# Halo rows copied by ScalarE, a tile per channel block, a fourth product buffer, a bank of its own for the back transposes and a new order, in a Restormer block

## The chip, the core and the metric

The kernel runs on one core of a Trainium2 chip. The metric is the device time of one launch in microseconds (us). Below, PE is TensorE, DVE is VectorE, ACT is ScalarE, POOL is GpSimd and SP is SyncE, as in the profile.

## The reference

The input `x` has 16 images of 128 channels by 96 by 96 pixels, all in float32. One transformer block is applied: attention over channels, and then a feed-forward network with a depthwise 3x3 convolution.

```python
xn1 = layernorm(x_hwc, ln1_w, ln1_b)                 # over the 128 channels of a pixel
x = x + attention(xn1, wq, wk, wv, wp)               # 8 heads; a 16x16 softmax per head, over all 9216 pixels
xn2 = layernorm(x_hwc, ln2_w, ln2_b)
h1 = einsum('bchw,oc->bohw', xn2, w_in)              # 128 -> 512 channels
h2 = conv2d(h1, w_dw, 3x3, padding=1, groups=512)    # depthwise: nine taps for each channel
x = x + einsum('bchw,oc->bohw', gelu(h2), w_out)     # 512 -> 128 channels
```

## The kernel before

Channels lie on the 128 partitions. An image is cut into 8 bands of 12 rows (1152 pixels), and a band into 3 units of 4 rows (384 pixels). Over the images run two normalising passes and the feed-forward network, all overlapped: while image i goes through the network, the second norm (`b`) of image i and the first norm (`a`) of image i+1 are prepared.

**A norm.** For each group of 4 x 128 pixels PE transposes pixels to partitions (`pT`, L495), DVE takes statistics (`st`, L501) and a variance (`ve`, L508), POOL raises it to the power -0.5 (`rstd`, L512), DVE makes a shift (`nb`, L516), ACT scales (`zT`, L535), and PE transposes back (`pB`, L571). ACT puts that into a padded image `xn` of 98 rows (L575 for `b`, with weight and bias columns; L579 for `a`, which also adds up the row sums of a unit). For pass `a` PE also accumulates the Gram matrix of `zT` (L545). Attention is then a chain of small steps on 128 x 128 matrices, since queries and keys are linear in that Gram matrix and in the pixel sums. The mixed result (`pm`, L456) is evacuated by ACT (L465), and a DMA that adds brings in `x` (L468).

**The network.** The 512 hidden channels are 4 blocks. For three of them, and in some bands for the fourth too, a band is a *job*: PE makes 14 rows of hidden values (`ph`, L756), ACT copies them into a padded tile `h1` (L761), and then the nine taps are shared out. ACT makes the first product into `h3` (L772) and two more into product tiles `pr` (also L772). DVE adds six taps into `h3`, one instruction of 1152 elements each (L776, called taps below). POOL issues two adding DMAs (L780): the first adds one `pr` tile to the other (the *pr add*), the second adds that sum to `h3` (the *h add*). ACT then applies the gelu (L784). For the fourth block (`PE_CHUNK`), in the bands that `by_pe` names, PE does the whole convolution instead, with nine matmuls for each unit on weights composed of `w_in` and a tap (`pc`, L829), and ACT applies the gelu from PSUM (L835). The output product (`po`, L852) adds up the four blocks, DVE adds it to `x` (L859), and SP stores.

The first two rows of a job's `h1` tile are the last two rows of the same block's job one band earlier. Before the change SP moves them by DMA: `keep_halo` (L752) saves rows 12 and 13 of `h1` into a tile `halo`, and `take_halo` (L749) brings them into rows 0 and 1 of another `h1` tile. Three `h1` tiles go round among all jobs.

**Buffers.** Of the 8 PSUM banks two hold `pT`, one the Gram matrix, and five go round among `ph`, `pc`, `po`, `pm` and `pB`. In SBUF there are 3 `pr` tiles, 9 `h3` tiles, 3 `zT` tiles, 6 band tiles `xb` and 2 band tiles `x1`.

**The order.** Each engine runs its instructions in the order written. That order comes from a planner in the kernel: each kind of work has a place number (`AT`, plus a step within a job) and rough durations, a list schedule over engines and buffers is played through, and the work is emitted in the order of its starts. It sets an order alone; the waits at run time are semaphores.

Of the kernel before, what the change touches and what calls it, by code (L numbers as in the profile page):

```python
# [9 lines left out]
F32 = mybir.dt.float32  # L10
# [15 lines left out]
AT = dict(  # L26
    weights=3.75, zeros=6.85, load_a=-9.5, forth_a=-1.65, stats_a=-6.65, variance_a=-4.05, power_a=1.6,
    shift_a=2.3, scaled_a=3.2, gram=2.15, back_a=-10.4, place_a=-5.35, attention=-6.3, mix=-6.6,
    residual=-4.9, mixed=-6.6, add_x=-2.1, forth_b=-5.75, stats_b=0.35, variance_b=-10.5, power_b=-15.05,
    shift_b=-8.65, scaled_b=0.5, back_b=-14.1, place_b=-5.75, take_halo=1.4, hidden=-0.6, kept=0.4,  # L30
    keep_halo=6.55, product=-2.75, products=1.25, add_last=-9.3, tap=3.3, add_first=11.25, gelu=-5.7,
    conv=2.8, conv_gelu=0.1, out=2.85, add=-1.65, store=1.5,
# [6 lines left out]
T_ADD, T_MOVE, T_HALO = 3100, 1800, 400  # L39
# [157 lines left out]
def tile_restormer_block(  # L197
# [33 lines left out]
    HP, WP = H + 2, W + 2  # L231
# [10 lines left out]
    p_h = ctx.enter_context(tc.tile_pool(name="p_h", bufs=5, space=PSUM))  # L242
    p_g = ctx.enter_context(tc.tile_pool(name="p_g", bufs=1, space=PSUM))

    xbs, x1s = {}, {}

# [22 lines left out]

    wqkT = const.tile([P, 2 * P], F32, name="wqkT")  # L270
# [8 lines left out]
    xns = [pad.tile([P, HP, WP], F32, tag=f"xn{k}", name=f"xn{k}") for k in range(min(B, 2))]  # L279
    small = ctx.enter_context(tc.tile_pool(name="small", bufs=4))  # L280
    xhp = ctx.enter_context(tc.tile_pool(name="xhp", bufs=3))
# [8 lines left out]
    h1s = [h1p.tile([P, BR + 2, WP], F32, name=f"h1_{k}") for k in range(H1_BUFS)]  # L290
    halos = [h1p.tile([P, 2, WP], F32, name=f"halo_{n}") for n in range(NCH) if n != PE_CHUNK]

    def interior(i, u):
        return xns[i % 2][:, 1 + u * UR : 1 + (u + 1) * UR, 1 : 1 + W]
# [4 lines left out]
    def x_unit(of, i, u):  # L299
# [3 lines left out]
    grams, sums, mats, h3s, staged = {}, {}, {}, {}, {}  # L303
    plan = Plan(
        tr=2, h=5, g=1, batch=4, zT=3, x1=X1_BUFS, xb=XB_BUFS, h1=H1_BUFS, pr=PR_BUFS, h3=H3_BUFS
# [3 lines left out]
    def at(kind, place):  # L309
        return place + AT[kind]  # L310

# [14 lines left out]

    def pe(ns, p, f, r, w):
        op("PE", ns, p, f, r, w, ns + 200 + SLACK, ns)
# [4 lines left out]
    def add(p, f, r, w):  # L333
        op("POOL", 950, p, f, r, w, 500 + SLACK, dma=T_ADD)
# [7 lines left out]
    def zeros(p):  # L342


        def around(t, r):
            for k in (0, r - 1) if r == HP else ():
                nc.gpsimd.memset(t[:, k, :], 0.0)
            for k in (0, WP - 1):
                nc.gpsimd.memset(t[:, :, k : k + 1], 0.0)

        for t, r in [(xns[0], HP)] + [(t, BR + 2) for t in h1s] + [(xn, HP) for xn in xns[1:]]:
            op("POOL", 1000, at("zeros", p), lambda t=t, r=r: around(t, r), [], [("w", "in")], 1200)

    def weights(p):

        mine = [("h3", ("weights", k)) for k in range(2)]
        v, banks = staged, iter(range(99))
# [13 lines left out]
        def transposed(parts, kept, gives):  # L371

            bank = ("h", ("weights", next(banks)))
            d = {}

            def forth():
                d["pt"] = p_h.tile([P, 4 * P], F32, tag="h", name=f"pw_{bank[1][1]}")
# [3 lines left out]
            pe(440, at("weights", p), forth, mine, [bank])  # L381
            dve(700, at("weights", p), lambda: kept(d["pt"]), [bank], [("w", g) for g in gives] + mine[1:])
# [6 lines left out]
        def biases():  # L389
            v["pc"] = p_h.tile([1, 2 * P], F32, tag="h", name="pc")  # L390
            nc.tensor.matmul(v["pc"], lhsT=b1, rhs=v["wqkT"], start=True, stop=True)

        def comp_parts(ts):
# [4 lines left out]

        op("ACT", 400, at("load_a", p), loads, [], mine, 900 + SLACK, dma=2 * T_MOVE)
        transposed(  # L400
# [6 lines left out]
            lambda pt: nc.vector.tensor_copy(winT.rearrange("p n c -> p (n c)"), pt), ["in"],  # L407
# [5 lines left out]
        for t0 in (0, 4, 8):  # L413
# [4 lines left out]
                lambda pt, ts=ts: nc.vector.tensor_copy(  # L418
                    comp[:, ts[0] : ts[-1] + 1, :].rearrange("p t c -> p (t c)"), pt[:, : len(ts) * P]
# [20 lines left out]
    def norm(i, second, place_of):  # L440
# [8 lines left out]
        def x2(s, u):  # L449
# [4 lines left out]
            def mix():  # L454
                pm = d["pm"] = p_h.tile([P, UT], F32, tag="h", name=f"pm_{i}_{u}")
# [26 lines left out]
        def pixels(s, q):  # L482
# [4 lines left out]
            pool, key_ = (p_h, "h") if early else (p_tr, "tr")  # L487
            by_dve = QT // 2 if early else 0

            def forth():  # L490
                d["pT"] = pool.tile([P, QT, P], F32, tag=key_, name=f"pT_{name}_{q}")
# [28 lines left out]
            def take_zT():  # L520
                zTs[q] = xhp.tile([P, QT, P], F32, tag="zT", name=f"zT_{name}_{q}")

            def also_scaled():
                for j in range(by_dve):
                    nc.vector.tensor_scalar(
                        zTs[q][:, j, :], d["pT"][:, j, :], d["mv"][:, j, 1:2], d["rstd"][:, j : j + 1],
# [3 lines left out]
            def scaled():  # L530
# [3 lines left out]
                for j in range(by_dve, QT):  # L534
                    nc.scalar.activation(  # L535
                        zT[:, j, :], d["pT"][:, j, :], AF.Identity,
# [3 lines left out]
            def gram():  # L540
                if q == 0:
                    grams[i] = p_g.tile([P, 4 * P], F32, tag="g", name=f"g_{i}")
                for t in tiles:
                    zt = zTs[q][:, t - tiles[0], :]
                    nc.tensor.matmul(  # L545
                        grams[i][:, :P], lhsT=zt, rhs=zt, start=(t == 0), stop=(t == NU * TPU - 1)
# [13 lines left out]
            if not second:  # L560
                pe(QT * 220, at("gram", s), gram, [(*zt, 0), (*zt, 1)], [("g", i)])

        def channels(s, u):
# [3 lines left out]
            def back():  # L567
                d["pB"] = p_h.tile([P, UT], F32, tag="h", name=f"pB_{name}_{u}")
                for j in range(TPU):
                    q, k = divmod(u * TPU + j, QT)  # L570
                    nc.tensor.transpose(d["pB"][:, j * P : (j + 1) * P], zTs[q][:, k, :], ident)  # L571
# [363 lines left out]
```

## Time and profile before

| what | value |
|---|---|
| median of three runs (lowest, highest) | 4548.23 us (4544.1, 4552.64) |
| the profiled execution's own time | 4542.75 us |
| its span | 4541.0 us |
| busy: PE, DVE, ACT, POOL | 4395.3, 4278.3, 4033.9, 1851.5 us |
| DMA queues' share of 16 engines: adding DMAs on POOL's queue, others | 68.0%, 14.3% |
| bytes moved by DMA | 806.84 MB |

Busy time on PE is the time covered by matmuls whose ends are modelled; successive ones overlap, so it overstates what PE needs. A row of a list of groups reads: source line, engine, operation, output and inputs, their shapes, count, then busy us, the mean ns of one, the idle time before it and what ended that. A row of a timeline reads: start in us, length in us, engine, line, operation, and a count where several like instructions in a row are merged. A row of the waits reads: who waited, for whom, total us, number of times, longest us.

### The profile page before, as it was taken

The numbers are of one execution on the slowest core, as the hardware profiler recorded it, in microseconds if no ns is written. First come the engines' busy times: TensorE is split into PE (matmuls) and PEld (weight loads), VectorE is DVE, ScalarE is ACT, GpSimd is POOL, SyncE is SP. The second block draws the span as 40 slices with busy tenths as digits, with TensorE's granted clock in tenths as the row PEclk, the third lists the DMA queues.
The fourth block names the chain that finished last, engine by engine and source line by source line (L and its number), as shares of the span: only waits on it lengthen the run. The fifth ranks groups of instructions, "written<-read, shape, count | busy, mean of one in ns | idle before, by whom it ended". The sixth has DMA issues, their size and how long they took to land.

```text
span 4541.0 us, 55504 instructions
## 1 busy us (share of the span) xinstructions
PE 4395.3 (97%) x17974; PEld 2798.1 (62%) x17974; DVE 4278.3 (94%) x5671; ACT 4033.9 (89%) x7100; POOL 1851.5 (41%) x1606
## 2 busy tenths in 40 slices
PE   7999999999999999999999999999999999999998
PEld 5666656666666665666666666666666656666554
DVE  6999999999999999999999999999999999999988
ACT  4889889899898998989999998998989989899876
POOL 2334434344344444434334343443444434344331
PEclk9999999999999999999999999999999999999999
DMA  2878888898898888888888888888988888888887
GB/s 71 175 172 182 175 181 187 177 195 175 174 195 181 191 173 180 192 170 182 184 183 188 179 187 178 183 178 174 198 179 174 183 182 185 184 183 173 172 171 159
DMA packets 279124, 806.84 MB, mean 178 GB/s; under 512 B 31920, under 2 KB 119344, under 8 KB 278832
## 3 DMA queue, kind: packets, MB, share of 16 engines
q0 software_dynamic: 142560, 583.99, 68.0%
q1 hardware_dynamic: 133920, 218.49, 14.3%
q8 instruction: 142, 2.33, 0.2%
q14 instruction: 150, 1.23, 0.1%
q10 hardware_dynamic: 2352, 0.81, 0.1%
HBM read 148.26 MB, written 75.50 MB: 49 GB/s over the span
## 4 chain that ended last, share of the span: by engine, by line
PE 35%; DMA 26%; DVE 15%; ACT 13%; issue 7%; POOL 4%; POOLq 0%; ACTq 0%; DVEq 0%
DMA pr<-pr 18%; DVE h L776 12%; PE pc L829 11%; PE po L852 8%; DMA h<-pr 7%; PE ph L756 6%; ACT pr L772 4%; PE g L545 2%; ACT h L772 2%; PE pm L456 2%; ACT zT_b L535 1%; DMA x<-in_x_dram 1%; ACT h L784 1%; ACT h L761 1%; PE pB_a L571 1%
## 5 line engine op out<-in xcount | busy, mean ns | idle before, releaser
L776 DVE SCALAR_TENSOR_TENSOR h<-h,dw,h 128x1152 f32<-128x1152 f32 x2612 | 3647.0, 1411 | 68.3 <-ACT h L772 57.9
L829 PE MATMUL pc<-xn,comp 128*128 128x384 f32 x4158 | 1490.3, 487 | 6.4 <-ACT x L465 2.1
L772 ACT ACTIVATE pr<-h,dw 128x1152 f32<-128x1152 f32 x868 | 1104.7, 1283 | 82.9 <-DMA pr<-pr 81.8
L852 PE MATMUL po<-h,woutT 128*128 128x384 f32 x3072 | 1124.6, 489 | 20.4 <-ACT h L784 12.1
L829 PEld LDWEIGHTS pc<-xn,comp 128*128 128x128 f32 x4158 | 766.1, 190 | 498.9 <-issue 8.2
L756 PE MATMUL ph<-xn,winT 128*128 128x384 f32 (+1 forms) x2610 | 1005.0, 503 | 30.9 <-ACT h L761 8.5
L780 POOL DMA_DIRECT2D h<-pr x434 | 395.6, 912 | 1509.7 <-DMA pr<-pr 420.3
L852 PEld LDWEIGHTS po<-h,woutT 128*128 128x128 f32 x3072 | 564.9, 190 | 399.2 <-ACT h L784 23.6
L756 PEld LDWEIGHTS ph<-xn,winT 128*128 128x128 f32 x2610 | 475.3, 190 | 369.8 <-issue 40.3
L784 ACT ACTIVATE h<-h 128x1152 f32<-128x1152 f32 (+1 forms) x437 | 516.9, 1183 | 188.9 <-DMA h<-pr 186.7
L761 ACT COPY h<-ph 128x384 f32<-128x384 f32 (+1 forms) x1305 | 616.5, 531 | 63.8 <-PE ph L756 59.5
L512 POOL TENSOR_TENSOR rstd_b<-ve_b,mhalf 128x4 f32<-128x4 f32 x288 | 506.7, 1769 | 374.5 <-DVE ve_b L508 357.2
L512 POOL TENSOR_TENSOR rstd_a<-ve_a,mhalf 128x4 f32<-128x4 f32 x288 | 505.5, 1755 | 319.0 <-DVE ve_a L508 300.7
L772 ACT ACTIVATE h<-h,dw 128x1152 f32<-128x1152 f32 x435 | 560.7, 1290 | 7.6 <-PE po L852 2.6
L780 POOL DMA_DIRECT2D pr<-pr x434 | 412.3, 950 | 319.6 <-ACT pr L772 274.0
L535 ACT ACTIVATE zT_b<-pT_b,nb_b,rstd_b 128x128 f32<-128x128 f32 x1142 | 438.7, 496 | 28.7 <-DVE nb_b L516 16.8
L535 ACT ACTIVATE zT_a<-pT_a,nb_a,rstd_a 128x128 f32<-128x128 f32 x1116 | 427.4, 490 | 18.8 <-DVE nb_a L516 10.5
L456 PE MATMUL pm<-xn,mwT 128*128 128x384 f32 x768 | 300.8, 493 | 11.6 <-ACT xn L575 4.3
L545 PE MATMUL g<-zT_a 128*128 128x128 f32 x2304 | 308.7, 278 | 0.0
L545 PEld LDWEIGHTS g<-zT_a 128*128 128x128 f32 x2304 | 285.6, 194 | 3.8
L575 ACT ACTIVATE xn<-pB_b,b,w 128x384 f32<-128x384 f32 x384 | 259.4, 706 | 15.8 <-PE pB_b L571 15.4
L501 DVE BATCH_NORM_STATS2 st_a<-pT_a 128x6 f32<-128x256 f32 x576 | 243.5, 426 | 20.3 <-PE pT_a L495 19.7
(97 smaller groups left out, 3173.0 us busy)
## 6 DMA issues: line engine op xcount, KB each, us to landing
pr<-pr POOLq DMA_DIRECT2D x434, 576.0 KB, 6.8
h<-pr POOLq DMA_DIRECT2D x434, 576.0 KB, 5.1
x<-in_x_dram SPq DMA_DIRECT2D x128, 576.0 KB, 5.7
out_dram<-x SPq DMA_DIRECT2D x127, 576.0 KB, 5.0
x<-in_x_dram POOLq DMA_DIRECT2D x122, 576.0 KB, 8.2
halo<-h SPq DMA_DIRECT2D x336, 98.0 KB, 4.2
h<-halo SPq DMA_DIRECT2D x336, 98.0 KB, 4.5
out_dram<-x SPq DMA_DIRECT2D x3, 192.0 KB, 1.9
```

What stands on the lines that cost most here:

```text
L456: nc.tensor.matmul(rows(pm), lhsT=mats[i][0], rhs=interior(i, u), start=True, stop=True)
L512: nc.gpsimd.tensor_tensor(rstd, d["ve"], mhalf, ALU.pow)
L535: nc.scalar.activation(zT[:, j, :], d["pT"][:, j, :], AF.Identity, bias=d["nb"][:, j : j + 1], scale=d["rstd"][:, j : j + 1],)
L545: nc.tensor.matmul(grams[i][:, :P], lhsT=zt, rhs=zt, start=(t == 0), stop=(t == NU * TPU - 1))
L756: nc.tensor.matmul(ph, lhsT=winT[:, n, :], rhs=xn[:, r0 + r : r0 + e, 1 : 1 + W], start=True, stop=True)
L761: nc.scalar.copy(h1_tile()[:, r:e, 1 : 1 + W], d.pop(("ph", r)))
L772: nc.scalar.activation(to, window(t), AF.Copy, scale=dw[:, n, t : t + 1])
L776: nc.vector.scalar_tensor_tensor(h3, window(t), dw[:, n, t : t + 1], h3, ALU.mult, ALU.add)
L780: nc.gpsimd.dma_start(out=to, in_=d["pr", t], accum_op=ALU.add)
L784: nc.scalar.activation(h3, h3, AF.Gelu)
L829: nc.tensor.matmul(d["pc"], lhsT=comp[:, t, :], rhs=xn[:, r0 + dy : r0 + dy + UR, dx : dx + W], start=(t == 0), stop=(t == 8),)
L852: nc.tensor.matmul(rows(d["po"]), lhsT=woutT[:, n, :], rhs=h3s[g, n][:, s * UR : (s + 1) * UR, :], start=(k == 0), stop=(k == NCH - 1),)
```

## The change

Six things are changed together.

1. **Halo rows by ACT.** Each channel block has an `h1` tile of its own (four in all). After a job, ACT copies rows 12 and 13 of the tile onto rows 0 and 1 of the same tile (336 copies of 2 x 96 elements). Both halo DMAs are gone, so SP only loads and stores. A row of the padded tiles has 97 elements in place of 98: the right pad of a row is the left pad of the next.
2. **Four product tiles** `pr` in place of three; five band tiles `xb` in place of six.
3. **Sums by a ones column.** `zT` has a 129th column of ones, so that the Gram matmul also gives the pixel sums. The placing of `pB` for pass `a` becomes a plain copy, and the accumulator reads and a DVE reduction per image go.
4. **Weight of the second norm folded into `w_in` and the composed weights** once at the start; the placing for pass `b` keeps one column (the bias) and loses the other.
5. **PSUM.** `pB` gets one bank of its own, and four banks go round among the rest.
6. **Another order, and fewer bands on PE.** New place numbers; the planner reckons an adding DMA's result 900 ns later than it did. PE convolves the fourth block in 73 of 128 bands (4 of every 7) in place of 77 (3 of every 5), so there are 439 jobs in place of 435.

```diff
-PE_BANDS = (1, 2, 4)
+PE_BANDS = (0, 2, 4, 6)
+PE_OF = 7
-X1_BUFS, XB_BUFS, H1_BUFS, PR_BUFS, H3_BUFS = 2, 6, 3, 3, 9
-IN_TURN = ("tr", "h3", "h1", "pr", "xb", "x1")
+H_BANKS = 4
+X1_BUFS, XB_BUFS, PR_BUFS, H3_BUFS, ZT_BUFS = 2, 5, 4, 9, 3
+IN_TURN = ("tr", "h3", "pr", "xb", "x1")
...
-    h1s = [h1p.tile([P, BR + 2, WP], F32, name=f"h1_{k}") for k in range(H1_BUFS)]
-    halos = [h1p.tile([P, 2, WP], F32, name=f"halo_{n}") for n in range(NCH) if n != PE_CHUNK]
+    h1s = [h1p.tile([P, (BR + 2) * WP + 2], F32, name=f"h1_{n}") for n in range(NCH)]
+    zT_bufs = [h1p.tile([P, QT, P + 1], F32, name=f"zT_{k}") for k in range(ZT_BUFS)]
+    def window(t, r, n, dx=0):
+        return t[:, r * WP + dx : (r + n) * WP + dx].rearrange("p (r w) -> p r w", w=WP)[:, :, :W]
...
-        op("POOL", 950, p, f, r, w, 500 + SLACK, dma=T_ADD)
+        op("POOL", 950, p, f, r, w, 1400 + SLACK, dma=T_ADD)
...
-                        grams[i][:, :P], lhsT=zt, rhs=zt, start=(t == 0), stop=(t == NU * TPU - 1)
+                        grams[i][:, : P + 1], lhsT=zt[:, :P], rhs=zt, start=(t == 0), stop=(t == NU * TPU - 1)
...
-                d["pB"] = p_h.tile([P, UT], F32, tag="h", name=f"pB_{name}_{u}")
+                d["pB"] = p_bk.tile([P, UT], F32, tag="bk", name=f"pB_{name}_{u}")
...
-                    nc.scalar.activation(interior(i, u), rows(d["pB"]), AF.Identity, bias=b2, scale=w2)
+                    nc.scalar.activation(interior(i, u), rows(d["pB"]), AF.Identity, bias=b2)
...
-                nc.scalar.activation(
-                    interior(i, u), rows(d["pB"]), AF.Identity, accum_out=sums[i][:, u : u + 1]
-                )
+                    nc.scalar.copy(interior(i, u), rows(d["pB"]))
...
-        def take_halo():
-            nc.sync.dma_start(out=h1_tile()[:, :2, :], in_=halos[n])
-        def keep_halo():
-            nc.sync.dma_start(out=halos[n], in_=h1_tile()[:, BR : BR + 2, :])
+        def halo():
+            nc.scalar.copy(window(h1_, 0, 2, 1), window(h1_, BR, 2, 1))
...
+        if to_halo:
+            act(t_copy(2 * W), at("halo", j), halo, h1[3:], h1[:1])
```

How the order moves is seen at three places. In the names, `pr_60_2_1` is product tile 1 of band 60, block 2; `h3_60_2` is that job's accumulator; `rstd_b7_15` is the power for group 15 of image 7 in pass `b`.

On POOL, about half way through the program, this stands before:

```order
L780 DMA pr_60_2_1_17406<-pr_60_2_2_17463 128x1152
L512 TENSOR_TENSOR rstd_b7_15_17500<-ve_b7_15_17494,mhalf_86 128x4
L780 DMA h3_60_2_17372<-pr_60_2_1_17406 128x1152
L780 DMA pr_60_3_1_17511<-pr_60_3_2_17529 128x1152
L512 TENSOR_TENSOR rstd_a8_16_17547<-ve_a8_16_17542,mhalf_86 128x4
L780 DMA h3_60_3_17446<-pr_60_3_1_17511 128x1152
```

and this after:

```order
L807 DMA pr_59_1_1_15571<-pr_59_1_2_15584 128x1152
L807 DMA h3_59_0_15436<-pr_59_0_1_15471 128x1152
L550 TENSOR_TENSOR rstd_b7_11_15613<-ve_b7_11_15597,mhalf_93 128x4
L550 TENSOR_TENSOR rstd_a8_16_15660<-ve_a8_16_15646,mhalf_93 128x4
L807 DMA pr_59_2_1_15643<-pr_59_2_2_15653 128x1152
L503 DMA x2_7_6_15619<-in_x_dram 128x1152
L807 DMA h3_59_1_15554<-pr_59_1_1_15571 128x1152
```

Before, a job's h add (`h3`) stands one to two rows behind its own pr add; after, the pr add of the next job has come in between. Over the whole program another job's pr add lies between a job's two adds in 13 of 434 jobs before, and in 365 of 438 after.

On DVE, in bands 56 and 57, this stands before (its first pair of taps starts at 2084.70 us of the profile):

```order
L776 SCALAR_TENSOR_TENSOR h3_57_0_16283<-h1_2_134,dw_98,h3_57_0_16283 128x1152
L776 SCALAR_TENSOR_TENSOR h3_56_2_16173<-h1_1_133,dw_98,h3_56_2_16173 128x1152
L516 SCALAR_TENSOR_TENSOR nb_a8_3_16401<-st_a8_3_16354,rstd_a8_3_16387 128x4
L776 SCALAR_TENSOR_TENSOR h3_57_0_16283<-h1_2_134,dw_98,h3_57_0_16283 128x1152
L501 BN_STATS st_b7_7_16412<-pT_b7_7_16371 128x6
L776 SCALAR_TENSOR_TENSOR h3_57_0_16283<-h1_2_134,dw_98,h3_57_0_16283 128x1152
L501 BN_STATS st_b7_7_16412<-pT_b7_7_16371 128x6
L776 SCALAR_TENSOR_TENSOR h3_57_0_16283<-h1_2_134,dw_98,h3_57_0_16283 128x1152
L508 TENSOR_SCALAR ve_b7_7_16434<-st_b7_7_16412 128x4
L776 SCALAR_TENSOR_TENSOR h3_57_1_16420<-h1_0_132,dw_98,h3_57_1_16420 128x1152 x2
```

and in band 56 after:

```order
L803 SCALAR_TENSOR_TENSOR h3_56_1_14763<-h1_1_138,dw_105,h3_56_1_14763 128x1152
L539 BN_STATS st_a8_7_14849<-pT_a8_7_14837 128x6
L803 SCALAR_TENSOR_TENSOR h3_56_0_14681<-h1_0_137,dw_105,h3_56_0_14681 128x1152
L554 SCALAR_TENSOR_TENSOR nb_b7_5_14860<-st_b7_5_14811,rstd_b7_5_14842 128x4
L539 BN_STATS st_a8_7_14849<-pT_a8_7_14837 128x6
L803 SCALAR_TENSOR_TENSOR h3_56_0_14681<-h1_0_137,dw_105,h3_56_0_14681 128x1152
L546 TENSOR_SCALAR ve_a8_7_14872<-st_a8_7_14849 128x4
L803 SCALAR_TENSOR_TENSOR h3_56_1_14763<-h1_1_138,dw_105,h3_56_1_14763 128x1152
L803 SCALAR_TENSOR_TENSOR h3_56_0_14681<-h1_0_137,dw_105,h3_56_0_14681 128x1152
```

Taps of two jobs alternate oftener, so a tap stands less often right behind a tap on the same `h3` tile (`x2`, as in the last row of the first piece): 275 such pairs in the whole program before, 123 after. Taps right behind a tap on another tile: 460 before, 634 after.

On ACT, in bands 61 to 63, this stands before around a gelu (`h3_62_0<-h3_62_0`):

```order
L772 ACTIVATE h3_62_2_17881<-h1_0_132,dw_98 128x1152
L835 ACT_TABLE_LOAD
L835 ACTIVATE h3_62_3_17886<-pc_62_0_17813 128x384
L772 ACTIVATE pr_62_1_2_17898<-h1_2_134,dw_98 128x1152
L761 COPY h1_1_133<-ph_63_0_2_17896 128x4x96
L761 COPY h1_1_133<-ph_63_0_6_17901 128x4x96
L784 ACTIVATE h3_62_0_17722<-h3_62_0_17722 128x1152
L772 ACTIVATE pr_62_2_1_17921<-h1_0_132,dw_98 128x1152
L761 COPY h1_1_133<-ph_63_0_10_17905 128x4x96
```

and in bands 60 and 61 after:

```order
L799 ACTIVATE pr_60_2_2_15954<-h1_2_139,dw_105 128x1152
L788 COPY h1_0_137<-h_1_77 128x4x96
L788 COPY h1_0_137<-h_3_79 128x4x96
L779 COPY h1_0_137<-h1_0_137 128x2x96
L788 COPY h1_0_137<-h_0_76 128x4x96
L799 ACTIVATE h3_61_0_15982<-h1_0_137,dw_105 128x1152
L779 COPY h1_1_138<-h1_1_138 128x2x96
L811 ACT_TABLE_LOAD
L811 ACTIVATE h3_60_0_15762<-h3_60_0_15762 128x1152
L799 ACTIVATE pr_61_0_1_16015<-h1_0_137,dw_105 128x1152
```

Two halo copies (L779) stand among the copies from PSUM now. Between a job's second `pr` product and its gelu stand 17 rows in the median before and 26 after.

More of the change, by code (lines that the diff above doesn't have):

```diff
@@ L310, in at, with bank @@
         return place + AT[kind]
+    def bank(key, n=4 * P):
+        return banks[plan.slot["h", key]][:, :n]
     def z_units(i, r0, r1):
@@ L356, in weights @@
         mine = [("h3", ("weights", k)) for k in range(2)]
-        v, banks = staged, iter(range(99))
+        v, names = staged, iter(range(99))
         def loads():
@@ L520, in take_zT @@
             def take_zT():
[L521 removed]
+                zTs[q] = zT_bufs[plan.slot["zT", (name, q)]]
             def also_scaled():
@@ L788, in conv_job @@
         left = [t for t in range(1, 9) if t not in dma_taps]
-        h1 = [("h1", jn, r) for r, _ in chunks]
+        h1 = [("h1", n, k) for k in range(4)]
         h3 = [("h3", jn, s) for s in range(UPB)]
-        after = []
-        if from_halo:
-            after = [("h1", jn, "halo")]
-            move(at("take_halo", j), take_halo, [("halo", n)], after, T_HALO)
         for k, (r, e) in enumerate(chunks):
@@ L850, in product @@
             if k == 0:
-                d["po"] = p_h.tile([P, UT], F32, tag="h", name=f"po_{g}_{s}")
+                d["po"] = bank(("out", g, s), UT)
             nc.tensor.matmul(
```

138 lines of the change are left out of this document (76 added, 62 removed).

## The prediction

> **What bounds the kernel now.** I read the page's head first, then the windows, then who waited for whom on DVE, and last what holds ACT and POOL.
>
> ```profile
> span 4541.0 us, 55504 instructions
> PE 4395.3 (97%) x17974; PEld 2798.1 (62%) x17974; DVE 4278.3 (94%) x5671; ACT 4033.9 (89%) x7100; POOL 1851.5 (41%) x1606
> 1000.00:1500.00 500.00, 490.95 (x2026) 314.03 (x2025) 478.12 (x632) 457.68 (x807) 211.44 (x178) 1.00 0.84 181
> 3500.00:4000.00 500.00, 488.07 (x1988) 307.69 (x1988) 471.73 (x622) 452.00 (x796) 206.50 (x177) 1.00 0.84 180
> ```
>
> The windows (PE, PE loads, DVE, ACT, POOL, granted clock, DMA share) are alike from 1000 to 4000 us: no stage stands out, and the granted clock is full. PE seems to lead, but its ends are modelled and overlap. What it needs is the spacing of its matmuls, which short and long rows of one line give:
>
> ```profile
> 2004.49 0.81 PE L829 MATMUL pc<-xn,comp 128*128 128x384 f32 x2
> 2009.00 2.10 PE L829 MATMUL pc<-xn,comp 128*128 128x384 f32 x6
> ```
>
> (2.10 - 0.81) / 4 = 0.3225 us for 384 columns. Against the 0.358 us that the page's group of `pc` has per matmul (1490.3 / 4158), PE is less full than 97% says; counted by spacings over all its groups I get about 4270 us (an estimate). So DVE, with 4278 us, is as full as PE, and a saving on PE alone buys only what DVE waits for. The sum therefore goes by DVE: its work, plus its 262.7 us of idle time (4541.0 - 4278.3):
>
> ```profile
> DVE h L776 <- ACT h L772: 57.9, 59, 4.8
> DVE nb_b L516 <- POOL rstd_b L512: 50.7, 56, 2.4
> DVE nb_a L516 <- POOL rstd_a L512: 39.9, 42, 2.1
> DVE st_a L501 <- PE pT_a L495: 19.7, 19, 5.5
> DVE st_b L501 <- PE pT_b L495: 15.3, 23, 3.9
> DVE x L859 <- PE po L852: 14.7, 21, 2.7
> ```
>
> Three quarters of the idle time, 198 us, are 57.9 us for a first product from ACT, 90.6 us for POOL's power, and 49.7 us for PE; the rest is the start and the attention chain. Why are ACT and POOL late, though both have idle time? Because each waits in order for adding DMAs:
>
> ```profile
> POOL h L780 <- DMA pr<-pr: 420.3, 109, 10.1
> ACT h L784 <- DMA h<-pr: 186.7, 150, 5.8
> ACT pr L772 <- DMA pr<-pr: 81.8, 80, 3.1
> POOL rstd_b L512 <- DVE ve_b L508: 357.2, 135, 12.0
> ```
>
> **The change, part by part.** *DVE's work.* Four more jobs are 24 more taps. Two rows of the timeline price a tap in its two positions; the order of before names the tiles of both:
>
> ```profile
> 2084.70 2.75 DVE L776 SCALAR_TENSOR_TENSOR h<-h,dw,h 128x1152 f32<-128x1152 f32 x2
> 2087.43 1.42 DVE L776 SCALAR_TENSOR_TENSOR h<-h,dw,h 128x1152 f32<-128x1152 f32 x1
> 2092.15 2.87 DVE L776 SCALAR_TENSOR_TENSOR h<-h,dw,h 128x1152 f32<-128x1152 f32 x2
> ```
>
> The first pair lies on two tiles (bands 57 and 56): 2.75 - 1.42 = 1.33 us from start to start. The last is on one tile: 1.45 us, so a tap that needs the one ahead starts 0.12 us later. New taps: 24 x 1.33 = +32 us. Pairs on one tile fall by 152: -152 x 0.12 = -18 us (ends: 0, if something else fills that gap, and -20). The 16 reductions that go are short, and I count them as nothing. DVE's work: +14 us.
>
> By the Trainium skill, VectorE: DVE Perf Modes, section "The DRAIN you can't avoid", the next instruction does not start until the pipe is empty, whatever it reads. By that rule the order of taps is worth nothing and the sum would be 18 us higher. The two pairs above disagree with it, so I keep the term.
>
> *PE.* The bands that PE no longer convolves drop 108 of 2079 `pc` matmuls, each two instructions: 216 x 0.3225 = -70 us. Their hidden rows come back as 4 matmuls of 384 columns and 8 of 480: 8 x 0.3225 + 16 x 0.3225 x 480 / 384 = +9 us. PE's need falls by 61 us. The 129th Gram column lies between nothing and the step to 256 columns:
>
> ```profile
> L545 PE MATMUL g<-zT_a 128*128 128x128 f32 x2304 | 308.7, 278 | 0.0
> L641 PE MATMUL g<-wqkT,gsb 128*128 128x256 f32 x32 | 9.6, 382 | 0.4 <-DVE srow L636 0.4
> ```
>
> One column of the 128 from 278 to 382 ns is 0.8 ns, 2 us over 2304; a whole step would be 104 ns, 240 us on PE. I take 2, since 480 columns cost more than 384 in proportion.
>
> *ACT.* These rows price it:
>
> ```profile
> 42.15 0.51 ACT L579 ACTIVATE xn<-pB_a 128x384 f32<-128x384 f32 x1
> 42.52 0.23 ACT L579 ACTIVATION_READ_ACCUMULATOR xn<-pB_a 128x1 f32 x1
> 42.61 0.84 ACT L535 ACTIVATE zT_a<-pT_a,nb_a,rstd_a 128x128 f32<-128x128 f32 x2
> L575 ACT ACTIVATE xn<-pB_b,b,w 128x384 f32<-128x384 f32 x384 | 259.4, 706 | 15.8 <-PE pB_b L571 15.4
> L465 ACT ACTIVATE x<-pm,d 128x384 f32<-128x384 f32 x366 | 216.1, 606 | 24.7 <-PE pm L456 23.2
> L761 ACT COPY h<-ph 128x384 f32<-128x384 f32 x1107 | 516.0, 516 | 59.1 <-PE ph L756 56.0 <-DVE x L859 1.3 <-DVE h L776 0.2
> L784 ACT ACTIVATE h<-h 128x1152 f32<-128x1152 f32 x434 | 515.6, 1188 | 188.6 <-DMA h<-pr 186.7
> L772 ACT ACTIVATE pr<-h,dw 128x1152 f32<-128x1152 f32 x868 | 1104.7, 1283 | 82.9 <-DMA pr<-pr 81.8
> L835 ACT ACTIVATE h<-pc 128x384 f32<-128x384 f32 x231 | 116.7, 507 | 25.2 <-PE pc L829 24.6
> ```
>
> An accumulator read delays the next instruction by 0.09 us (42.52 to 42.61): 384 of them, -35. One operand column less is 706 - 606 = 100 ns: 384 of them, -38. A halo copy is 192 elements from SBUF. The gelu's slope over the PSUM form, (1188 - 516) / 768 = 0.875 ns, leaves 0.18 us of fixed time, so 0.35 us alone; ACT's neighbours overlap by some 0.1 us (0.51 long, 0.37 to the next start above). 336 x 0.25 = +84 us, with ends 57 (0.17 each, the slope alone) and 118 (nothing overlaps). Four jobs more, each, with 0.1 off every length, three products of 1.18, a gelu of 1.09 and three copies of 0.42 less three gelus from PSUM of 0.41: 4 x 4.7 = +19. ACT's work: +30 us, into 507 us of idle time. It shows only if the waits do not go.
>
> *DMA.* The answer on the tile `halo` lists nobody who waited for it, and the kernel's issues by size follow:
>
> ```profile
> L749 SPq DMA_DIRECT2D h<-halo x336: 464/465/1912, 120.0 to 4501.4; - x168
> who waited for it (us, times):
> ...
> pr<-pr POOLq DMA_DIRECT2D x434, 576.0 KB, 6.8
> h<-pr POOLq DMA_DIRECT2D x434, 576.0 KB, 5.1
> ...
> halo<-h SPq DMA_DIRECT2D x336, 98.0 KB, 4.2
> ```
>
> So the 672 halo transfers free no engine directly when they go; they are 66 of 807 MB, and the adding DMAs gain eight of 576 KB. SP's queue keeps only loads and stores, and no load stands behind a halo's wait any more. I take nothing for it.
>
> *The waits.* Here is the gain. With the fourth `pr` tile, the pr add of the next job goes out between a job's two adds. Before, POOL mostly issued the h add right behind and stood for the 6.8 us of landing. This takes most of the 420.3 us, during which powers were queued. I let half of DVE's 90.6 us go, -45; the rest is the power's own length, which the order leaves about two taps from `ve` to `nb` as before. ACT's gelus stand 26 rows behind the second product in place of 17, which covers landing, and the fourth tile covers the 81.8 us. Of ACT's 268.5 us of waits for DMA most go; late next on ACT is PE (59.5 us for `ph`). Two thirds of DVE's 57.9 us, -38. PE has 61 us less to do: half of 49.7, -25. Against these stands the single bank for `pB`, halo copies ahead of a first product, five `xb` tiles: new waits, +10, between 0 and the 84 us of the copies.
>
> Sum: 14 - 45 - 38 - 25 + 10 = -84 us. Against the execution's own 4542.75 us that is 4459 us. The median of the runs shown, 4548.23, is 5 us above that execution, and carries over. A change under 0.2%, 9 us, could not be told from none here.
>
> **The rivals.** *The waits only move.* DVE waits as long as before, now for ACT behind its halo copies or for later landings: 4543 + 14 = 4557. For it: all engines are near full, and each window has the same 4 to 6% of DVE idle. Against: the largest wait is taken away at its source.
>
> *The single bank stalls PE*, and the kernel is slower. A unit's `pB` can start only when ACT has placed the one ahead. Before, five banks let this run:
>
> ```profile
> L571 PE MATMUL pB_a<-ident,zT_a 128*128 128x128 f32 x1152 | 186.6, 279 | 12.4 <-ACT xn L579 3.6 <-ACT h L761 3.3 <-DVE ve_a L508 2.7
> L571 PE MATMUL pB_b<-ident,zT_b 128*128 128x128 f32 x1152 | 182.4, 276 | 14.8 <-ACT h L761 8.0 <-ACT x L465 2.4 <-DVE zT_b L525 1.7
> ```
>
> There are 768 such units. If each stood 0.25 us, PE would lose 192 us and keep 131 more than it gains: about 4675. It decides from 61 / 768 = 0.08 us per unit, where PE's gain is gone. Against it: in the order after, only 12 of 767 successive units have under 1.2 us of matmuls between them, 199 before.
>
> *Nearly all of DVE's steady waits go.* Then the 198 us of the six rows go: 4543 + 14 - 198 = 4359. Against: DVE would be busy 98% of the span (4292 / 4359), and POOL's power would never be late.
>
> *Taps cost the same in any order*, each starting when the one ahead has ended: 4459 + 18 = 4477. The two pairs speak against it; it lies within the forecast's own range, with 0.05 of its chance.
>
> *The DMAs stay the pace.* The adding DMAs hold 68.0% of the engines and are eight more; if their landing grew with the overlap of two, the gelus would wait as they do now. ACT's 186.7 us would stay, with it the 38 and half of the rest: 4543 + 14 - 35 = 4522.
>
> **How the numbers follow.** The forecast, between 4410 and 4505, gets 0.60; that DMAs stay the pace 0.13; that waits only move 0.09; the stall of PE 0.09; nearly no waits 0.09. To leave out no more than 2 in 10, the range goes from 4395 to 4535: it takes in the DMA case, and leaves out the two that are not faster and the far end of the best. If the halo copies and the 18 us all go the wrong way, the forecast is 4459 + 18 + 74 = 4551, so the upper end is not out of its reach. Faster: 0.60 + 0.13 + 0.09 = 0.82, less 0.01 for the DMA case's end, 0.81; same: two thirds of the second, 0.07; slower: 0.12.
>
> **What would show it.** In the profile after: POOL's wait of the h add for the pr add well under 200 us; ACT's waits for `h<-pr` and `pr<-pr` together under 130; DVE's for `rstd` near 45 and for ACT's first product near 20; DVE's busy time about 4292 and its idle time near 165 (262.7 - 108 + 10); PE's busy time some 60 lower; a halo copy of 0.35 us with no long wait ahead of it. Wrong would make it: PE waiting for the placing of `pB`, ACT waiting at the halo copy for DVE's last tap, a Gram matmul nearer 382 than 278 ns, or loads that come late with five `xb` tiles.

## The result and the profile after

| | before | after |
|---|---|---|
| median of 4 runs each (lowest, highest) | 4546.16 us (4543.82, 4552.64) | 4418.30 us (4415.02, 4421.42) |
| ratio, 95% interval | | 0.9716 [0.970, 0.9733] |
| the profiled execution's own time | 4542.75 us | 4421.42 us |

The change makes the kernel 128 us faster by the medians, and 121.3 us by the two profiled executions. The forecast was 4459 us, a gain of 84. Line numbers have moved: the taps are L803 now (L776 before), the products L799, the copies from PSUM L788, the gelu L811, POOL's adds L807, the power L550, the statistics L539, the placings L613 and L615, the output product L876 and its addition to `x` L883. The tiles that share a PSUM bank are all called `h` in the rows, as `h1` and `h3` are.

The head of the page after:

```profile
span 4419.5 us, 53360 instructions
PE 4309.8 (98%) x17782; PEld 2750.3 (62%) x17782; DVE 4271.7 (97%) x5681; ACT 4059.8 (92%) x7071; POOL 1884.1 (43%) x1620
```

DVE's busy time is 6.6 us less than before (4278.3) and its idle time 147.8 us (4419.5 - 4271.7) where it was 262.7. Those two differences, 6.6 and 114.9, are the whole 121.5 us of the span. Nearly all of the gain is waiting that DVE no longer does. The same two windows as before show it as a steady state, not as a stage:

```profile
1000.00:1500.00 500.00, 496.21 (x2041) 315.19 (x2041) 487.66 (x646) 470.73 (x819) 222.17 (x183) 1.00 0.82 172
3500.00:4000.00 500.00, 491.91 (x2029) 313.47 (x2028) 487.85 (x642) 468.50 (x818) 220.36 (x184) 1.00 0.82 171
```

DVE (third figure) goes from 478 and 472 us of each 500 to 488, ACT (fourth) from 458 and 452 to 471 and 469. Who waited for whom, first DVE, then ACT, then POOL:

```profile
DVE nb_b L554 <- POOL rstd_b L550: 32.0, 33, 1.6
DVE nb_a L554 <- POOL rstd_a L550: 25.7, 31, 0.9
DVE x L883 <- PE h L876: 18.1, 16, 6.1
DVE st_a L539 <- PE pT_a L533: 11.4, 15, 3.4
DVE st_b L539 <- PE pT_b L533: 5.7, 9, 1.4
DVE st_a L539 <- PE h L533: 5.1, 8, 1.1
DVE h L803 <- ACT h L799: 1.0, 4, 0.4
...
ACT h L788 <- PE h L783: 68.8, 127, 2.0
ACT h L811 <- DMA h<-pr: 68.6, 63, 7.8
ACT pr L799 <- DMA pr<-pr: 30.7, 30, 3.6
...
POOL pr L807 <- ACT pr L799: 611.8, 223, 9.0
POOL h L807 <- DMA pr<-pr: 16.8, 5, 5.9
```

DVE's wait for a first product from ACT is gone (57.9 to 1.0), that for the power is down by a third (90.6 to 57.7), that for PE by a fifth (49.7 to 40.3). POOL's wait of the h add for the landing of its own pr add falls from 420.3 to 16.8; POOL stands for the second product instead (274.0 before). ACT's gelus wait 68.6 us for the h add in place of 186.7, its products 30.7 for a free tile in place of 81.8. These rows of the groups, of after, price the changed instructions:

```profile
L803 DVE SCALAR_TENSOR_TENSOR h<-h,dw,h 128x1152 f32<-128x1152 f32 x2636 | 3651.3, 1405 | 5.4 <-ACT h L799 1.0
L583 PE MATMUL g<-zT 128*128 128x129 f32 x2304 | 304.8, 274 | 0.2 <-DVE zT L563 0.2
L609 PE MATMUL pB_b<-ident,zT 128*128 128x128 f32 x1152 | 192.4, 274 | 5.6 <-ACT xn L613 4.3 <-ACT zT L573 1.0
L613 ACT ACTIVATE xn<-pB_b,b 128x384 f32<-128x384 f32 x384 | 242.7, 632 | 24.4 <-PE pB_b L609 23.4
L779 ACT COPY h<-h 128x192 f32<-128x192 f32 x336 | 134.2, 399 | 0.0
```

The Gram matmul with its 129th column takes 274 ns, as a back transpose of 128 columns does beside it. A halo copy takes 0.399 us and has no wait ahead of it. With one bank PE stands 4.3 us in all ahead of `pB_b` for the placing before it.

### The profile page after: what moved, and what is told of

It is laid out like the page before. It is cut to its first block, busy times and chain, and to the rows that moved or that the text cites. A ratio compares the mean times of both kernels' runs of the same rounds, so it can differ in the third digit from the quotient of the medians.

```text
span 4419.5 us, 53360 instructions
## 1 busy us (share of the span) xinstructions
PE 4309.8 (98%) x17782; PEld 2750.3 (62%) x17782; DVE 4271.7 (97%) x5681; ACT 4059.8 (92%) x7071; POOL 1884.1 (43%) x1620
## 3 DMA queue, kind: packets, MB, share of 16 engines
q1 hardware_dynamic: 37152, 151.01, 9.4%
## 5 line engine op out<-in xcount | busy, mean ns | idle before, releaser
L803 DVE SCALAR_TENSOR_TENSOR h<-h,dw,h 128x1152 f32<-128x1152 f32 x2636 | 3651.3, 1405 | 5.4 <-ACT h L799 1.0
L853 PE MATMUL h<-xn,comp 128*128 128x384 f32 x3942 | 1422.7, 486 | 8.2 <-ACT x L500 5.0
L799 ACT ACTIVATE pr<-h,dw 128x1152 f32<-128x1152 f32 x876 | 1131.1, 1301 | 31.3 <-DMA pr<-pr 30.7
L876 PE MATMUL h<-h,woutT 128*128 128x384 f32 x3072 | 1116.1, 492 | 41.3 <-ACT h L788 17.7
L783 PE MATMUL h<-xn,winT 128*128 128x384 f32 (+1 forms) x2634 | 1034.2, 500 | 5.7 <-ACT h L859 2.4
L853 PEld LDWEIGHTS h<-xn,comp 128*128 128x128 f32 x3942 | 719.4, 189 | 465.7 <-issue 17.1
L876 PEld LDWEIGHTS h<-h,woutT 128*128 128x128 f32 x3072 | 562.6, 192 | 400.9 <-ACT h L788 27.9
L807 POOL DMA_DIRECT2D h<-pr x438 | 408.1, 932 | 845.8 <-issue 154.3
L788 ACT COPY h<-h 128x384 f32<-128x384 f32 (+1 forms) x1317 | 655.0, 532 | 90.8 <-PE h L783 68.8
L807 POOL DMA_DIRECT2D pr<-pr x438 | 404.3, 923 | 752.0 <-ACT pr L799 611.8
L550 POOL TENSOR_TENSOR rstd_b<-ve_b,mhalf 128x4 f32<-128x4 f32 x288 | 524.1, 1820 | 380.4 <-DVE ve_b L546 354.1
L550 POOL TENSOR_TENSOR rstd_a<-ve_a,mhalf 128x4 f32<-128x4 f32 x288 | 509.2, 1773 | 388.4 <-DVE ve_a L546 376.1
L783 PEld LDWEIGHTS h<-xn,winT 128*128 128x128 f32 x2634 | 474.7, 190 | 304.6 <-issue 35.9
L811 ACT ACTIVATE h<-h 128x1152 f32<-128x1152 f32 x441 | 529.4, 1201 | 71.4 <-DMA h<-pr 68.6
L799 ACT ACTIVATE h<-h,dw 128x1152 f32<-128x1152 f32 x439 | 569.8, 1298 | 4.9 <-PE h L876 1.1
L573 ACT ACTIVATE zT<-pT_b,nb_b,rstd_b 128x128 f32<-128x128 f32 x1132 | 438.8, 510 | 14.6 <-DVE nb_b L554 13.6
L573 ACT ACTIVATE zT<-pT_a,nb_a,rstd_a 128x128 f32<-128x128 f32 x1080 | 417.5, 508 | 22.3 <-DVE nb_a L554 19.4
L613 ACT ACTIVATE xn<-pB_b,b 128x384 f32<-128x384 f32 x384 | 242.7, 632 | 24.4 <-PE pB_b L609 23.4
L539 DVE BATCH_NORM_STATS2 st_b<-pT_b 128x6 f32<-128x256 f32 x566 | 236.2, 420 | 6.2 <-PE pT_b L533 5.7
```

The costliest lines, as they stand in the source:

```text
L550: nc.gpsimd.tensor_tensor(rstd, d["ve"], mhalf, ALU.pow)
L573: nc.scalar.activation(zT[:, j, :P], d["pT"][:, j, :], AF.Identity, bias=d["nb"][:, j : j + 1], scale=d["rstd"][:, j : j + 1],)
L783: nc.tensor.matmul(rows(ph), lhsT=winT[:, n, :], rhs=window(xn, r0 + r, e - r, 1), start=True, stop=True)
L788: nc.scalar.copy(window(h1_, r, e - r, 1), rows(d.pop(("ph", r))))
L799: nc.scalar.activation(to, shifted(t), AF.Copy, scale=dw[:, n, t : t + 1])
L803: nc.vector.scalar_tensor_tensor(h3, shifted(t), dw[:, n, t : t + 1], h3, ALU.mult, ALU.add)
```

## The experiments

Twelve kernels ran, each beside the kernel before, whose median was 4547.8 to 4551.7 us beside them. Ratios are to it, with 95% intervals. Nearly any edit makes the planner write a new order, so that a run shows an edit together with the order that it brings. "Crossed" is the number of jobs with another job's pr add between their two adds, as in the part on the order.

### The fourth product tile, the places and the planner's number

Three product tiles in the changed kernel:

```diff
-X1_BUFS, XB_BUFS, PR_BUFS, H3_BUFS, ZT_BUFS = 2, 5, 4, 9, 3
+X1_BUFS, XB_BUFS, PR_BUFS, H3_BUFS, ZT_BUFS = 2, 5, 3, 9, 3
```

> The changed kernel with three pr tiles in place of four; all place numbers as they are, and the planner makes its order for three. In that order another job's pr add lies between a job's two adds in 12 of 438 jobs (365 in the changed kernel, 13 before). Theory A, that the gain comes from POOL and ACT no longer standing at the landing of adding DMAs, which the fourth tile allows: POOL waits for the pr add to land 300 us or more again, ACT waits for DMA 200 us or more, and the time is 4490 to 4560 us. Rival B, that the relief of PE by four bands makes the gain, and rival C, that the halo DMAs' going makes it: both stay as they are here, so under 4440 us.

4619.44 us, 1.0161 [1.0144, 1.0178]: the right direction, and far more than expected. Without the fourth tile the rest of the change makes the kernel slower. The head of its page, and its waits:

```profile
PE 4385.6 (95%) x17782; PEld 2785.8 (60%) x17782; DVE 4319.2 (94%) x5681; ACT 4098.2 (89%) x7071; POOL 1878.2 (41%) x1620
```

```profile
DVE x L883 <- PE h L876: 91.4, 70, 13.5
DVE h L803 <- ACT h L799: 46.7, 42, 5.6
DVE nb_a L554 <- POOL rstd_a L550: 25.0, 29, 2.0
...
DVE nb_b L554 <- POOL rstd_b L550: 23.8, 24, 2.1
...
POOL h L807 <- DMA pr<-pr: 396.1, 106, 8.6
...
ACT h L811 <- DMA h<-pr: 96.1, 68, 7.3
...
ACT pr L799 <- DMA pr<-pr: 35.5, 46, 1.9
```

POOL stands 396.1 us for its own landings again, since 12 of 438 jobs are crossed. But DVE's wait for the power is 48.8 us here, less than the 57.7 of after: the landings do not reach DVE by way of the power. What DVE waits for more is PE and ACT: 91.4 us for the output product (+73) and 46.7 for a first product (+46). The links between POOL and these waits are not shown: ACT's own waits for landings come to 131.6 us here (96.1 + 35.5), 32 more than after and well under the 200 that were expected. PE, too, is busy 75.8 us longer for the same 17782 matmuls (4385.6 against 4309.8), at a granted clock of 0.977 in place of 0.993, so a slower PE may be a part of the loss; how large a part was not measured. DVE's busy time is 47.5 us higher too; 403 pairs of taps on one tile in place of 123, at the 0.11 us measured below, are 31 of them.

The place numbers of before, with four tiles and with three:

```diff
-    weights=0.9, zeros=6.55, load_a=-14.05, forth_a=-8.8, ...
+    weights=3.75, zeros=6.85, load_a=-9.5, forth_a=-1.65, ...
...
```

> The changed kernel with the place numbers of before (the halo copy at its new number), four pr tiles, 73 bands on PE, all else as changed. Its order crosses the adds of two jobs in 253 of 438 jobs. Theory A, that the fourth tile does it whatever the place numbers are: 4430 to 4480 us. Rival D, that the new place numbers do most of it: 4500 to 4560 us.

> As the run with the place numbers of before, and three pr tiles: the numbers were made for three, so this asks for the tile without the bad fit of the first run (4619 us). Its order crosses the adds in 11 of 438 jobs. Theory A: POOL waits for the pr add's landing 300 us or more, and the time is 50 us or more over that of the run with four tiles, 4500 to 4560. If the first run's loss came only from place numbers that do not suit three tiles: within 30 us of the run with four tiles.

4516.01 us, 0.9929 [0.9913, 0.9946], with 253 jobs crossed; and 4632.24 us, 1.0186 [1.0171, 1.0202], with 11. The first lies where the rival put it that the places do most of it; the second lies the 50 us or more above it that the theory asked for, but 72 us above the range that it gave. Together with after and the run above:

| | three `pr` tiles | four `pr` tiles | the tile's worth |
|---|---|---|---|
| places of before | 4632.2 | 4516.0 | -116 |
| new places | 4619.4 | 4418.3 | -201 |
| the new places' worth | -13 | -98 | |

The new places are worth little without the tile (the intervals of the two runs with three tiles overlap), and the tile less without them. But the corner with neither is 84 us slower than the kernel before, though it has the rest of the change. Two runs looked for that: six band tiles `xb` again, and then 77 bands on PE as well.

```diff
-X1_BUFS, XB_BUFS, PR_BUFS, H3_BUFS, ZT_BUFS = 2, 5, 4, 9, 3
+X1_BUFS, XB_BUFS, PR_BUFS, H3_BUFS, ZT_BUFS = 2, 6, 3, 9, 3
...
-PE_BANDS = (0, 2, 4, 6)
-PE_OF = 7
+PE_BANDS = (1, 2, 4)
+PE_OF = 5
...
```

> The changed kernel with the place numbers of before, three pr tiles and six xb tiles, as before had them; 73 bands on PE. The run with five xb tiles took 4632 us, 84 us more than the kernel before, although ACT's and PE's work is no heavier for it. If the missing xb tile makes those 84 us (the fourth pr tile was paid for with it): 4545 to 4575 us. If not, they lie in the bands or in the buffers: within 20 us of 4632.

> The same with 77 bands on PE: of the change this leaves the halo by ACT, the ones column, the folded weight, the bank for pB and the planner's later landing. Theory A, that these are worth little: within 30 us of the kernel before, 4520 to 4580. Rival C, that they carry part of the gain: under 4510. If with three pr tiles the new shares or the own bank cost time: over 4590.

4631.62 us, 1.0185 [1.0168, 1.0202], and 4626.90 us, 1.0169 [1.0154, 1.0184]: neither is the cause. What was left were the halo copies and ACT's other edits, the banks, and the planner's numbers. So the one number that says when an adding DMA's result may be used was put into the kernel before, and taken out of the changed one:

```diff
-        op("POOL", 950, p, f, r, w, 500 + SLACK, dma=T_ADD)
+        op("POOL", 950, p, f, r, w, 1400 + SLACK, dma=T_ADD)
```

The diff is that of the kernel before; that of the changed kernel is the reverse.

> The kernel before with one number of its planner changed: the result of an adding DMA is reckoned 1400 ns after its end in place of 500, as in the changed kernel. It moves the order alone; three product tiles, five shared banks and the halo DMAs stay. Taps right behind a tap on the same tile become 342 (275 before), jobs whose two adds have another job's pr add between them 9 (13 before). Theory: the old place numbers suit only the costs that they came with, so this number accounts for a good part of the 79 us by which the parts without new places and without the fourth tile were slower: 4590 to 4640 us, DVE's waits for the first product and for the power up by 40 us or more together. Rival: it is the halo copies and other ACT work that those places cannot bear: then this stays at 4540 to 4560 us.

> The changed kernel with the planner's result of an adding DMA 500 ns after its end, as before, in place of 1400; new places, four product tiles, halo by ACT. 360 of 438 jobs have another job's pr add between their two adds (365 in the changed kernel), 144 pairs of taps on the same tile (123). Theory: with the fourth tile the crossing of the adds stays, so the time stays near 4418, between 4410 and 4440 us, and DVE's wait for the first product under 10 us. Rival: the later result is what keeps the gelus and first products from waiting: then ACT's wait for the h add goes back from 68.6 to 120 us or more and the time is 4450 us or more.

In the kernel before, the number alone costs 117 us: 4666.40 us, 1.026 [1.0243, 1.0278], more than was expected. DVE's wait for a first product doubles, while that for the power stays (94.2 us), and POOL's for its landings grows:

```profile
DVE h L776 <- ACT h L772: 117.6, 55, 16.6
DVE nb_b L516 <- POOL rstd_b L512: 49.8, 53, 2.3
DVE nb_a L516 <- POOL rstd_a L512: 44.4, 42, 3.3
...
POOL h L780 <- DMA pr<-pr: 470.0, 122, 8.6
...
ACT h L784 <- DMA h<-pr: 91.1, 70, 6.7
```

ACT's gelus wait only half as long for the h add (91.1 in place of 186.7), and the kernel is slower all the same, so that wait alone does not tell what an order is worth. The halo copies are not needed to explain a slow kernel with three tiles: in the kernel before, a planner that expects late landings writes a slower order. The slow corner itself was not run with the earlier number, so that it has the same cause is likely and not shown. In the changed kernel the same number gains 56 us: without it 4474.12 us, 0.9833 [0.9819, 0.9848], outside the first theory's bounds. There 360 jobs are still crossed, and yet the gelus wait longer:

```profile
ACT h L811 <- DMA h<-pr: 129.4, 118, 7.9
```

That is the rival's case. Crossing the adds is therefore not all of the gain; what stands between the h add and the gelu seems to count too, though the median distance of second product and gelu is 26 rows in both. DVE waits 19 us more for PE's transposes of pass `a` (30.2) and its busy time is 10.5 us higher.

The fourth tile alone, or the new places alone, were not run in the kernel before: beside its six band tiles a fourth product tile does not fit in SBUF, and its buffers do not suffice for the new places. So the three edits' worths are known only inside the changed kernel.

### The bands on PE

```diff
-PE_BANDS = (0, 2, 4, 6)
-PE_OF = 7
+PE_BANDS = (1, 2, 4)
+PE_OF = 5
```

> The changed kernel with the bands of PE as before (3 of 5, 77 bands, 435 jobs). PE needs 61 us more, DVE has 24 taps (32 us) less. Theory A: PE, at 4270 us of need, becomes the fuller engine, and the time rises by 15 to 45 us to 4435 to 4465. Rival B, the gain is PE's relief: the time goes up by 60 us or more, 4480 and over. If DVE's work alone sets the time: 4390.

4467.75 us, 0.9822 [0.9808, 0.9837]: 49 us above after, a little over what was expected. DVE's waits:

```profile
DVE x L883 <- PE h L876: 32.3, 29, 7.2
...
DVE st_a L539 <- PE pT_a L533: 21.4, 24, 3.4
DVE h L803 <- ACT h L799: 14.1, 18, 3.4
DVE st_b L539 <- PE pT_b L533: 12.7, 21, 2.5
```

DVE has 24 fewer taps and is busy 7.4 us less (4264.3), but waits 31 us more for PE in these three rows and 13 more for a first product. Four bands on PE, reckoned at 61 us of PE's need, come out as about 50 us of time. The order has moved too (263 jobs crossed), so not all of it need be PE's work.

### The taps' order

Two taps of a job as one piece of work for the planner, so that they always stand together:

```diff
-        for k, t in enumerate(left):
-            dve(t_dve(BR * W), at("tap", j + STEP["tap"] * k), lambda t=t: tap(t), h1, h3, True)
+        for k in range(0, len(left), 2):
+            dve(2 * t_dve(BR * W), at("tap", j + STEP["tap"] * k), lambda k=k: [tap(t) for t in left[k : k + 2]], h1, h3, True)
```

> The changed kernel with two successive taps of a job emitted as one piece of work, so that 1342 taps stand right behind a tap on the same h3 tile (123 in the changed kernel) and 173 behind a tap on another (634). By the price of 0.12 us that two rows of the profile before gave, DVE's busy time grows by 1219 x 0.12 = 146 us, less what small instructions between taps cover, so to 4350 to 4420 us; the time is 4480 us or more. If the next instruction always waits for the pipe to empty whatever it reads, DVE's busy time stays within 20 us of 4272, and the time changes only by what the coarser pieces do to the waits.

4816.15 us, 1.0588 [1.0572, 1.0603]. The order is far worse in other ways too (DVE idle 410 us), so the time says little on the taps. DVE's busy time says it:

```profile
PE 4463.9 (93%) x17782; PEld 2777.8 (58%) x17782; DVE 4404.6 (91%) x5681; ACT 4096.6 (85%) x7071; POOL 1771.2 (37%) x1620
```

4404.6 - 4271.7 = 132.9 us for 1342 - 123 = 1219 more pairs on one tile, 0.109 us each, with the same instructions. The tap in the group has hardly become longer (1413 against 1405 ns): its start comes later. The traces show it pair by pair, when the taps are matched with the order: in this run the 1342 taps behind one on the same tile start 1.445 us after it in the median, the 173 behind one on another tile 1.335; in the kernel before the two are 1.453 and 1.329. In the program each tap on the same tile waits by a semaphore for the one ahead.

### ACT's work and the halo's way

The halo rows by a DMA from SP again, in the changed kernel; and, in a second run, ACT's two savings at the placings taken back with the order of after (the sums go to a column that nobody reads, and the scale is a column of ones):

```diff
-            nc.scalar.copy(window(h1_, 0, 2, 1), window(h1_, BR, 2, 1))
+            nc.sync.dma_start(out=h1_[:, 1 : 1 + 2 * WP - 1], in_=h1_[:, BR * WP + 1 : (BR + 2) * WP])
...
-            act(t_copy(2 * W), at("halo", j), halo, h1[3:], h1[:1])
+            move(at("halo", j), halo, h1[3:], h1[:1], 400)
```

```diff
+    spare = const.tile([P, 1], F32, name="spare")
...
-                    nc.scalar.activation(interior(i, u), rows(d["pB"]), AF.Identity, bias=b2)
+                    nc.scalar.activation(interior(i, u), rows(d["pB"]), AF.Identity, bias=b2, scale=ones)
...
-                    nc.scalar.copy(interior(i, u), rows(d["pB"]))
+                    nc.scalar.activation(interior(i, u), rows(d["pB"]), AF.Identity, accum_out=spare)
```

> The changed kernel with its 336 halo copies given back to SP as one DMA each, from rows 12 and 13 of the tile onto rows 0 and 1 of the same tile (193 elements a row). ACT has 84 us less to do, the DMA engines 336 small transfers more. Theory A: the halo is a matter of indifference, 4405 to 4440 us. Rival C, that the way of the halo rows makes a large part of the 128 us: over 4460 us, with waits for the halo on ACT or PE.

> The changed kernel in the same order, with the placing of pB as it was: for pass a with an accumulator output (written to a spare column, used by nobody), for pass b with a second operand column (ones). ACT has 384 x 0.09 + 384 x 0.10 = 73 us more to do, nothing else changes. If ACT has time to spare, as its wait for PE and for DMA in the changed profile says (over 250 us idle in all): within 15 us of 4418. If ACT is the engine that the others wait for by now: 4450 us or more.

By DMA: 4424.74 us, 0.973 [0.9715, 0.9744], against 0.9716 [0.970, 0.9733] of after, no difference that can be told. ACT is busy 68.7 us less (3991.1), 0.20 us for each of the 336 copies. Less work on ACT and more DMAs together come out at nothing that can be told, in an order of its own (318 jobs crossed); by the run that follows, the work saved on ACT may be worth some 19 us, and the DMAs that come back may cost as much (an estimate: 68.7 us at 17 us for each 62.4). With the work back: 4436.23 us, 0.9753 [0.9738, 0.9767], about 17 us above after. Its page:

```profile
PE 4318.6 (97%) x17782; PEld 2748.4 (62%) x17782; DVE 4273.7 (96%) x5681; ACT 4122.2 (93%) x7455; POOL 1877.0 (42%) x1620
```

62.4 us more on ACT, at the same place in each unit and with the same order, cost about a quarter of themselves. ACT's work is neither free nor what sets the pace.

### The bank of its own

```diff
-H_BANKS = 4
+H_BANKS = 5
...
-                d["pB"] = p_bk.tile([P, UT], F32, tag="bk", name=f"pB_{name}_{u}")
+                d["pB"] = bank((name, u, "back"), UT)
...
```

> The changed kernel with pB back among the shared PSUM banks, five of them; place numbers as they are. Its order is much like the changed one (365 crossed adds, 93 taps behind a tap on the same tile in place of 123). Theory A: the bank of its own is worth little, 4405 to 4440 us. If a bank apart is what keeps PE from standing: 4450 us or more, with PE's or ACT's waits at pB grown by 40 us.

4422.48 us, 0.9721 [0.9706, 0.9735]: within the intervals of after. The bank neither stalls PE nor gives anything that can be told.

None of the twelve beats the changed kernel.

## Why the prediction was right, and where its working was not

The direction and the kind of gain were right: waits, not work. The sum missed by 38 us (4459 against 4421.4 of the profiled execution). Three of its terms gave too little gain, DVE's work by 20.6 us, the first product by 18.9 and the new waits with the rest of the idle time by 25.7; two gave too much, the power by 12.1 and PE by 15.6. That the sum came as near as it did is in part luck: these errors offset each other.

**DVE's work: +14 forecast, -6.6 measured.** The steps for new taps and fewer pairs were right in kind: the pair's price, 0.12 us from two rows, is 0.109 over 1219 pairs. With it falls the rival that taps cost the same in any order. The Trainium skill, VectorE: DVE Perf Modes, section "The DRAIN you can't avoid", taken as the prediction took it, disagrees with this measurement, which decides; the section also says that an instruction that is not held starts earlier, which agrees with the 1.33 us of taps on two tiles (a tap is 1.41 us long). Its section "Two Vector instructions with no wait between them" is, by its title, for instructions without a wait; these taps wait by a semaphore for the one ahead, so it gives no reason for the 0.109 us. What the sum missed is that nearly every DVE instruction came out a little shorter. In the kernel before, the groups of the taps and of the variances are:

```profile
L776 DVE SCALAR_TENSOR_TENSOR h<-h,dw,h 128x1152 f32<-128x1152 f32 x2612 | 3647.0, 1411 | 68.3 <-ACT h L772 57.9
...
L508 DVE TENSOR_SCALAR ve_b<-st_b 128x4 f32<-128x4 f32 x288 | 49.1, 171 | 0.5
```

The tap goes from 1411 to 1405 ns, which is 16 us over 2636 of them: 24 more taps and fewer pairs add only 4.3 us to the group. The variance of pass `b` goes from 171 to 162. They are nearly as short with the halo by DMA (1407 and 161), so the halo's DMAs are not the cause. They are longer again (1410 and 166) in the run with old places, three product tiles and six band tiles. It stays open.

**First product: -38 forecast, -56.9 measured.** The step "two thirds" was too timid: the wait goes wholly. It is 46.7 us with three tiles, 9.1 with the earlier planner's number and 28.0 with the old places. The three together take it away.

**The power: -45 forecast, -32.9 measured.** The size was near, but the step that led to it failed: "this takes most of the 420.3 us, during which powers were queued". With three tiles POOL stands as long as before for its landings (396.1), and DVE's wait for the power is 48.8 us all the same. Why it fell from 90.6 is not shown; it stays at 94.2 in the kernel before with the later landings planned.

**PE: -25 forecast, -9.4 measured** in the rows named. But taking the four bands back costs 49 us, 31 of it in waits for PE. So the bands' worth seems under-sized, and something else took part of it back in these rows; what that was is open. PE's busy time, with its modelled ends, fell by 85.5 us where some 60 were forecast.

**New waits: +10 forecast, -15.7 measured**, the largest term of the miss. The rest of DVE's idle time, outside the rows of the sum, falls by 15.7 us ((262.7 - 198.2) - (147.8 - 99.0)); in the attention chain DVE's wait for POOL falls from 5.3 to 0.8 us, that for a PSUM copy from 5.5 to 3.1, and the 2.4 ahead of the reduction go with it; the start gives nothing, since 6.1 us for a norm's weight are new there.

**ACT: +30 forecast, +25.9 measured** (4033.9 to 4059.8). A halo copy is 0.399 us long in place of 0.35 and takes 0.20 of ACT in place of 0.25; taking the kept weight column away saves 74 ns at each placing (706 to 632) in place of 100. That this work hides was mostly right: a quarter of it shows.

The halo's two transfers of 98 KB for each of 336 are 67 MB, not 66 (the queue that carried them moved 218.49 MB before and 151.01 after). Of the rivals, "the single bank stalls PE" is refuted by the run on the bank, and "the DMAs stay the pace" by ACT's wait for the h add, which would have stayed at 186.7 us and came to 68.6; nearly all waits going was half right, as DVE's waits for the product, the power and PE fell from 198.2 to 99.0 us. What the prediction did not cost at all is the planner's number: 56 us of the gain hang on it, and in the kernel before it would have been a loss of 117.

## What to carry to other kernels

Count a wait's way to the engine that sets the time before crediting it: when POOL stood for its landings again, with three tiles, DVE waited longer for ACT's products and PE's outputs, not for the power that was queued on POOL. A buffer and an order must be judged together: the fourth tile gave 201 us with the places and the planner's number that use it, 116 with other places, and those same numbers without the tile made the kernel 1.6 to 2.6% slower than before. Put dependent instructions apart on DVE where the order is free: each pair cost 0.11 us here.

## What had not been expected of the hardware

- A 129th column in a matmul's moving operand cost nothing that shows: 274 ns against 278 for 128 columns before and 274 for the 128 of the back transposes beside it, and eight in a row take 1.05 us against 1.06 before.
- A copy of 192 elements from SBUF to SBUF on ACT, 0.399 us in the mean, is not far below the 0.520 of a copy of 384 from PSUM.
- Orders that cross the adds of two jobs did not lengthen the pr add: its median landing fell from 6.8 us before to 5.4, while the h add's rose from 5.1 to 6.2. With three tiles, which hardly cross and have no halo DMAs either, they are 6.3 and 5.0. After, and then with three tiles:

```profile
pr<-pr POOLq DMA_DIRECT2D x438, 576.0 KB, 5.4
h<-pr POOLq DMA_DIRECT2D x438, 576.0 KB, 6.2
...
pr<-pr POOLq DMA_DIRECT2D x438, 576.0 KB, 6.3
h<-pr POOLq DMA_DIRECT2D x438, 576.0 KB, 5.0
```

- The granted clock of TensorE was lower in slow orders: 0.993 after, 0.977 with three tiles, 0.973 with taps in pairs, 0.981 with the later result in the kernel before; but 0.989 in one (old places, three tiles, six band tiles, 77 bands) that was as slow as those. How much time it cost was not measured.
